# A graph network with one-hot matmuls: groups paired in TensorE's order, and 64 instead of 60 source blocks in slots

## The chip, the cores and the metric

The kernel runs on one core of a Trainium2 chip. The metric is the device time of one execution in microseconds (us). Five engines work side by side, each in its own order: TensorE (PE; its weight loads are PEld), VectorE (DVE), ScalarE (ACT), GpSimd (POOL) and SyncE (SP). SP, ACT and POOL also start DMA transfers.

## What is computed

The graph has 12500 nodes with 128 features and 200000 edges, each with 16 attributes and a type. Cut to what matters:

```
# gated layer, messages along src -> dst
msg      = x[src] @ W_msg.T + b_msg + edge_embed[type]
messages = segment_sum(msg, dst)
x        = layernorm(x + gru(messages, x))
# three layers of the second net, messages along dst -> src, plus a self loop per node
for i in 0..2:
    ee  = ea @ enc_w + enc_b
    agg = segment_sum(concat(h[dst], ee), src)      # layer 0 adds the two instead
    h   = relu(bn(agg @ w1 + b1)) @ w2 + b2         # relu between layers
out = layernorm(x + h)
```

The weights can be moved behind the sums, so each of four layers comes down to one sum of node rows over edges, `acc[target] += x[source]`, and small dense products per node. What differs between the layers is only the direction and the dense part. The graph is known only at run time, so the kernel sorts the edges on the chip first.

## The kernel before, in words

**Blocks, buckets and slots.** Nodes are in 98 blocks (NB) of 128. The edges from one source block to one target block are a bucket, some 21 edges. A bucket has SL = 32 slots. Node rows are kept as three bf16 parts side by side, 384 columns (H3). For a target block `o` the slots of its buckets are worked through in tiles of 128 slots, four buckets to a tile, and in groups of TG = 3 tiles:

- *Pick* (line 1550): four matmuls with 32 columns of weights each, one per bucket, put the source rows of the slots into PSUM: `pg`, three banks. The one-hot matrix `g` says which row a slot wants. `psg` holds two such buffers.
- *Copy* (1559, or 1556 and 1557 together): ACT, in the first layer also DVE, moves the group from PSUM to `e` in bf16. `edges` holds three such tiles.
- *Add* (1507, `scatter`): a matmul per tile with the one-hot `st` of the targets adds the slots to the 128 target rows in the bank `acc`.

The first layer (`i == 0`, the gated one) has all 98 buckets in slots: 25 tiles, 9 groups. The later layers take only the first `ic` source blocks this way, and the edges from all source blocks beyond are *fetched*: `fetch` (1484) has POOL gather `rt` tiles of 128 rows from the table in device memory with an indirect DMA each, and `scatter_rows` (1515) adds each with one matmul. The pairs (ic, rt) are in PLANS: list C, (72, 5), for layer 1; list D, (60, 7), for layers 2 and 3. `rb`, the fetched tiles in flight, is 14 minus the number of the table's resident tiles (`xf`).

**What doesn't fit.** A bucket with more than 32 edges, or a target block with more than `rt * 128` edges from beyond, has some left over. Up to 8 of the former go to the end of the last fetched tile (`held`). The rest are written to a list (C or D), and before the layer `spill` (called at 1605, body in `added`, 596 to 665) adds the list's edges in groups of 128: a hardware loop over a count read at run time, in which a position is loaded, then a place, a key and two rows are gathered, then the sum is scattered back. List A holds the overfull buckets of the first layer.

The lists are written by `Listed`. `mark` (937) counts and writes the first two rounds of list A. `rest` (1049) is a hardware loop with `count["A"][0]` turns, and each turn does one `round` (eight columns of list A) and one `more` (eight columns of list C and eight of list D). The count is the largest need of any one block, in eights:

```
V.tensor_add(self.two[:NB, q + 1:q + 2], left[:NB, 0:1], left[:NB, 1:2])   # what block and plan leave over
V.tensor_tensor(c[:, 0:1], c[:, 0:1], most, op=OP.max)                      # most = max over blocks + 7
V.tensor_single_scalar(c[:, 0:1], c[:, 0:1], 3, op=OP.logical_shift_right)  # in eights
```

`write` (1042) issues eight indirect DMAs for each eight columns. Inside the loop all three writes of a turn use the same pair of tiles `rowi` and `val`, so DVE may fill them again only once the eight DMAs have landed. All engines meet at the entry of such a loop and at the end of each turn.

**Attributes.** `attributes` gathers the 16 attributes of each edge, by the block of its `src`, 17 indirect DMAs a block (736), into one of four buffers `eat`, and `add_up` splits them in bf16 parts (753 to 757), builds a one-hot (758), and adds them up on PE (764). It is a generator, moved on by the sorting at first and then by the layers 0 and 1 at fixed places (`pace`).

**Dense part.** After the last add of a block, `finish` adds `acc` to `s` with three DVE operations (1527 to 1529; a fourth, 1531, in layer 0), and after every second block puts a generator `gru` or `gin` on the list `work`. `tick` moves it on by one stage per group: transposes of `s` (1369, 1372 or 1415), then matmuls with the weights (1385 to 1387, or 1424 and 1425), then those of 1435.

**Order.** The setup up to the lists has DVE's, ACT's and PE's orders by hand in most parts. In the layers each engine's order is chosen by the compiler's scheduler from its own estimates of time; POOL's and SP's always are. In the program text a group is picked, and then the group before it is added.

Of the kernel before, what the change touches and what calls it, by code (L numbers as in the profile page):

```python
# [8 lines left out]
F32 = mybir.dt.float32  # L9
BF16 = mybir.dt.bfloat16  # L10
# [3 lines left out]
OP = mybir.AluOpType  # L14
# [3 lines left out]
E = 200000  # L18
H = 128
# [4 lines left out]
P = 128  # L24
NB = -(-N // P)
NPAD = NB * P
H3 = 3 * H
# [21 lines left out]


IC = 72
CELL = 7
PLANS = (Plan("C", IC, 5, False, CELL + IC // 4), Plan("D", 60, CELL, True, 0))
RT = sum(p.rt for p in PLANS)
TW = CELL + IC // 4 + PLANS[0].rt
OV = 8
REF = 1 << 19

# [21 lines left out]
LW = 175  # L80
GL = 8
GE = 2
assert EP * EC == E and all(p.ic % (4 * TG) == 0 for p in PLANS)
assert LCAP >= E and (LCAP + 8 * P) // P % LW == 0
assert LR * RW >= E + NB * NQ * (RW - 1) and LR % 2 == 0

# [2 lines left out]
def gnn_kernel(ctx: ExitStack, tc: tile.TileContext, x, xT, src, dst, ea, et, w_msg, w_ihT, w_hhT, b_msg,  # L89
# [23 lines left out]
    def ctile(shape, name, dtype=F32):  # L113
        return const.tile(shape, dtype, name=name)
# [10 lines left out]
    before = ctile([P, P], "before")  # L125
    V.tensor_scalar(before, diff, 0.0, None, op0=OP.is_gt)
    after = ctile([P, P], "after")
    V.tensor_scalar(after, diff, 0.0, None, op0=OP.is_lt)
    ident = diff
    V.tensor_scalar(ident, diff, 0.0, None, op0=OP.is_equal)  # L130
    identb = ctile([P, P], "identb", BF16)
# [253 lines left out]
    pre = ExitStack()  # L385
    pst = pre.enter_context(tc.tile_pool(name="pst", bufs=2, space=PSUM))
    pss = pre.enter_context(tc.tile_pool(name="pss", bufs=2, space=PSUM))
    kp = pre.enter_context(tc.tile_pool(name="keysA", bufs=1, side="right"))
# [78 lines left out]
    nidentb = ctile([P, P], "nidentb", BF16)  # L467
    V.tensor_scalar(nidentb, ident, -1.0, None, op0=OP.mult)


# [274 lines left out]
    def add_up(b, at):  # L745
        own = owp.tile([P, EA], F32, name="own")
        nc.sync.dma_start(own, ovfe[b * P:(b + 1) * P, :])
        oh = eop.tile([P, P, WC], BF16, name="eoh")
        a3 = attr3[b % 2]
        for f0 in range(0, P, P // 2):  # L750

            if f0 == 0:
                A.copy(a3[:, :, 1:EA], at)
                V.tensor_sub(at, at, a3[:, :, 1:EA])
            else:
                A.copy(a3[:, :, EA:EA + DE], at)
# [12 lines left out]
        V.tensor_add(own[:, 1:], own[:, 1:], ps[:, EA + DE:EW])  # L769
        yield  # L770
        own6 = owp.tile([P, 6, EA], BF16, name="own6")
        pieces6(own6, own, lambda a, b: own6[:, a:b, :], lambda t, n: t[:, None, :].to_broadcast([P, n, EA]))
        pt = psa.tile([P, 1024], BF16, name="acc") if early else psd.tile([P, 1024], BF16, name="d")
# [444 lines left out]
    hs.close()  # L1218
    kb.close()

    eap = ctx.enter_context(tc.tile_pool(name="attrs", bufs=4))
    owp = ctx.enter_context(tc.tile_pool(name="own", bufs=2))
    eop = ctx.enter_context(tc.tile_pool(name="attr1h", bufs=1))
    attr3 = [eop.tile([P, WN, EW], BF16, name=f"attr3{i}") for i in range(2)]
# [78 lines left out]
    ep = ctx.enter_context(tc.tile_pool(name="edges", bufs=3))  # L1303
# [55 lines left out]
    def gru(i, b0, s):  # L1359
# [4 lines left out]
        if c1 < 2 * P:  # L1364
            V.memset(xt, 0.0)
        nc.sync.dma_start(xt[:, :c1], xT[:, b0 * P:b0 * P + c1])
        pt = psd.tile([P, 512], F32, name="d")
        for k in range(2):
            T.transpose(pt[:, k * P:(k + 1) * P], s[:, k, 0:H], ident)
            c6 = dq.tile([P, 6, NTX], BF16, name="c6")  # L1370
            pieces6(c6, s[:, k, H:], lambda a, b: c6[:, a:b, :], lambda t, n: t[:, None, :].to_broadcast([P, n, NTX]))
            T.transpose(pt[:6 * NTX, 256:384].bitcast(BF16)[:, k * P:(k + 1) * P],
                        c6.rearrange("p a b -> p (a b)"), identb)
        sT = dq.tile([P, 2 * P], F32, name="sT")
        V.tensor_copy(sT, pt[:, :256])
        cT = dq.tile([6 * NTX, 2 * P], BF16, name="cT")
# [71 lines left out]
                yield from layernorm(y, *whole, True)  # L1448


    def layer(i, pace):

        cells_only = i == 0
        p = None if cells_only else PLANS[i > 1]
# [45 lines left out]
        last = None  # L1500
        sums = {}

        def scatter(o, st, e, k):
            for j in range(min(TG, tiles - TG * k)):
                t = TG * k + j
                m = P if t < NTL - 1 else P // 2
                T.matmul(sums[o][:, :wid], st[:m, :, cell + t], e[:m, j, :wid], start=(t == 0),  # L1507
                         stop=(t == tiles - 1), skip_group_check=True)

        def scatter_rows(o, st, j0, j1):  # L1510
            if j0 >= rt:
                return
            j1 = min(j1, rt)
            for j in range(j0, j1):
                T.matmul(sums[o][:, :H3], st[:, :, row + j], fetched[o][:, j, :], start=False, stop=False,  # L1515
                         skip_group_check=True)
            if j1 == rt:
                del fetched[o]

        def finish(o):  # L1520
            nonlocal s
# [10 lines left out]
            if o % 2:  # L1532
                work.append((gru if cells_only else gin)(i, o - 1, s))

        for o in range(NB):
            g, st = ready.pop(0)
            pieces = one_hots(o + 1) if o + 1 < NB else iter(())
# [4 lines left out]
            for k in range(groups):  # L1542
# [17 lines left out]
                if cells_only:  # L1560
                    t = TG * k
                    V.tensor_tensor(e[:m, :n, H3:], iota[:m, None, :NTX].to_broadcast([m, n, NTX]),
                                    typecol[:m, o, t:t + n, None].to_broadcast([m, n, NTX]), op=OP.is_equal)
                if k == 0:
                    if last:
                        if not cells_only:
                            scatter_rows(o - 1, last[1], 2 * groups - 4, rt)
                        scatter(*last)
                        finish(o - 1)
                else:  # L1570
                    if k == 1:
                        sums[o] = psa.tile([P, 512], F32, name="acc")
                    scatter(*last)
                    if not cells_only and k > 1:
                        scatter_rows(o, st, 2 * k - 4, 2 * k - 2)
                if k == 0 and not cells_only:
                    fetch(o + rb - 1)
                last = (o, st, e, k)
                tick()
                next(pieces, None)  # L1580
                if cells_only:
                    if k in (2, 6):
                        next(chunk, None)
                    if o >= 8 and k == 4:
                        next(row_slots, None)
                if pace(o, k):
                    next(attr, None)
            for _ in pieces:
                pass
        if not cells_only:  # L1590
            scatter_rows(NB - 1, last[1], 2 * groups - 4, rt)
        scatter(*last)
        finish(NB - 1)
        while work:
            tick()
        for _ in row_slots or ():
# [2 lines left out]
    for i in range(4):  # L1599
        if i:  # L1600
            X = xtiles(-(-PLANS[i > 1].ic // XC))
            for k in range(len(X)):
                (nc.sync if k % 2 else nc.scalar).dma_start(
                    X[k], tables[i][k * XC * P:(k + 1) * XC * P, :].rearrange("(b p) f -> p b f", p=P))
        for _ in spill(i):
            pass
        layer(i, (lambda o, k: k in (1, 5) or k == 3 and o % 5, lambda o, k: k == 3)[i] if i < 2
              else lambda o, k: False)
        if i == 1:
            for _ in attr:  # L1610
                pass
# [38 lines left out]
```

## Time and profile before

Three runs: median 5781.7 us, 5779.15 to 5783.01. The profiled execution took 5775.4 us, its span 5773.6 us.

| | us |
|---|---|
| sort and lists, up to the first `finish` | 1318.5 |
| layer 0, first to last `finish` | 1487.8 (98 blocks, 15.34 each) |
| layer 1 | 1068.2 (11.01 each) |
| layer 2 | 897.7 (9.25 each) |
| layer 3 | 882.3 (9.10 each) |

The stretches run from the first to the last start of line 1529 in each layer, as the timeline has them; the 30 to 41 us between two layers are in none of the rows. Over the span PE is busy 80%, DVE 61%, ACT 59% and POOL 67%. A row of the timeline gives its start in us, its length in us, engine, line, operation, tiles, count, and in brackets the idle time before it with what ended it.

### The profile page before, as it was taken

The page shows a single profiled execution, that of the slowest core. Times are in us where ns is not written, and L with a number is a line of the kernel's source. Part 1 is how long each engine was busy: PE and PEld are TensorE (multiplying, and loading weights), DVE is VectorE, ACT ScalarE, POOL GpSimd, SP SyncE. Part 2 cuts the span into 40 slices and gives each one's busy share as a digit, 9 for nine tenths or more (in the row PEclk, how much of TensorE's full clock was granted, in tenths as well). Part 3 has the DMA queues.
Part 4 walks back from the last instruction along what each step waited for, and adds up shares of the span by engine and source line. Part 5 has one row for each costly group of instructions (what it writes and reads, how often), then busy time and mean ns, then how long its engine had stood idle before and what let it go on. Part 6 is the DMA issues. An engine that isn't in the chain of part 4 may idle for free. (4 is left out here: it accounts for less than half of the span.)

```text
span 5773.6 us, 117175 instructions
## 1 busy us (share of the span) xinstructions
PE 4590.5 (80%) x45358; PEld 2754.9 (48%) x45358; DVE 3500.1 (61%) x9502; ACT 3396.2 (59%) x4901; POOL 3855.7 (67%) x3716
## 2 busy tenths in 40 slices
PE   3874252118999999999799989988999997999998
PEld 3774122104444444444355555554555554555555
DVE  9987679837887777777444444443444443444444
ACT  7772131106666666666566666665666665666665
POOL 1001878866676767766677777775777776777776
PEclk9755555559999999999899999999999998999999
DMA  5101130012333333323444444445555555555554
GB/s 65 38 1 33 47 90 7 7 35 74 102 89 86 89 89 101 89 85 89 144 128 125 134 121 129 127 115 166 157 160 158 159 155 167 156 156 156 156 157 131
DMA packets 539973, 616.43 MB, mean 107 GB/s; under 512 B 130184, under 2 KB 458028, under 8 KB 538760
## 3 DMA queue, kind: packets, MB, share of 16 engines
q1 hardware_dynamic: 327302, 373.36, 20.1%
q0 software_dynamic: 148192, 202.82, 14.3%
q10 hardware_dynamic: 63914, 32.71, 2.7%
q8 instruction: 355, 5.82, 0.4%
q14 instruction: 210, 1.72, 0.1%
HBM read 519.72 MB, written 88.82 MB: 105 GB/s over the span
## 5 line engine op out<-in xcount | busy, mean ns | idle before, releaser
L1559 ACT CAST e<-g 128x1152 bf16<-128x1152 f32 (+1 forms) x2058 | 2216.2, 1091 | 907.7 <-PE g L1550 766.3
L1484 POOL DMA_INDIRECT x<-table,rowcol x1862 | 1861.2, 1000 | 641.4 <-issue 600.5
L736 POOL DMA_INDIRECT eat<-in_ea,eidcol x1666 | 1794.8, 1077 | 640.0 <-issue 495.0
L1550 PE MATMUL g<-x,g 128*32 128x384 bf16 x28420 | 1688.1, 333 | 93.6 <-DVE e L1557 54.2
L1507 PE MATMUL acc<-e,s 128*128 128x384 bf16 (+2 forms) x7154 | 1646.8, 344 | 116.9 <-ACT e L1556 51.6
L1507 PEld LDWEIGHTS <-s 128*128 128x128 bf16 (+1 forms) x7154 | 939.2, 153 | 745.4 <-issue 470.4
L1550 PEld LDWEIGHTS <-g 128*32 128x32 bf16 x28420 | 613.0, 96 | 911.6 <-issue 711.1
L1474 DVE TENSOR_TENSOR s<-iotas,outcol 128x704 bf16<-128x704 bf16 (+2 forms) x1568 | 838.7, 544 | 0.3 <-PE acc L1507 0.3
L1471 DVE TENSOR_SCALAR g<-inr,pidx 128x1920 bf16<-128x1920 bf16 (+2 forms) x392 | 329.9, 842 | 793.9 <-PE g L1550 685.7
L1515 PE MATMUL acc<-x,s 128*128 128x384 bf16 x1862 | 512.4, 335 | 155.5 <-DMA x<-table,rowcol 153.9
L1556 ACT CAST e<-g 128x768 bf16<-128x768 f32 x392 | 317.2, 809 | 192.9 <-PE g L1550 126.6
L567 PE MATMUL acc<-ot,oa 125*98 125x101 bf16 x1600 | 295.7, 358 | 126.8 <-ACT ot L548 95.6
L1527 DVE TENSOR_TENSOR s<-s,acc 128x128 f32<-128x128 f32 x392 | 112.5, 287 | 408.5 <-PE acc L1507 402.7
L1515 PEld LDWEIGHTS <-s 128*128 128x128 bf16 x1862 | 271.8, 146 | 176.1 <-issue 147.5
L567 PEld LDWEIGHTS <-oa 125*98 125x98 bf16 x1600 | 292.1, 277 | 129.6 <-issue 87.5
L548 ACT ACTIVATE ot<-dbb,bias 125x160 bf16<-125x160 bf16 (+2 forms) x1078 | 332.4, 406 | 16.4 <-PE acc L567 8.2
L800 POOL IOTA num<- 98x2176 uint16 x1 | 1.9, 1947 | 462.4 <-DMA sortedB<-keyB 462.4
L1427 ACT ACTIVATE gates<-d,shift,scale 128x256 f32<-128x256 f32 x294 | 150.1, 561 | 245.7 <-PE d L1425 245.7
L1557 DVE CAST e<-g 128x384 bf16<-128x384 f32 x392 | 216.6, 553 | 75.2 <-ACT e L1556 70.8
L1440 DVE TENSOR_TENSOR n<-d,b 128x256 f32<-128x256 f32 x98 | 41.6, 424 | 279.7 <-PE d L1435 278.6
L764 PEld LDWEIGHTS <-eoh 128*128 128x128 bf16 x1666 | 116.8, 163 | 197.3 <-DVE eoh L758 172.2
L316 DVE TENSOR_TENSOR keyA<-keyA 128x1024 f32<-128x1024 f32 (+1 forms) x178 | 190.9, 1072 | 15.4 <-ACT keyA L332 12.8
(423 smaller groups left out, 4761.8 us busy)
## 6 DMA issues: line engine op xcount, KB each, us to landing
inr<-inrow SPq DMA_DIRECT2D x196, 480.0 KB
inr<-inrow SPq DMA_DIRECT2D x98, 784.0 KB
inr<-inrow SPq DMA_DIRECT2D x98, 576.0 KB
x<-table,rowcol POOLq DMA_INDIRECT x1862
table<-x SPq DMA_DIRECT2D x147, 192.0 KB
eat<-in_ea,eidcol POOLq DMA_INDIRECT x1666
s<-ovf SPq DMA_DIRECT2D x147, 128.0 KB
ovf<-n SPq DMA_DIRECT2D x98, 128.0 KB
```

What stands on the lines that cost most here:

```text
L548: A.activation(self.ot[j % 2][:, b, :ENDS[j] - c0], dbb[:, c0:ENDS[j]], AF.Sign, bias=self.bias[:, b:b + 1], scale=-1.0)
L567: T.matmul(cps[:NB, :NB + NQ - 1], self.oa[c // HC][:, :, c % HC], self.ot[j % 2][:, :, c - (ENDS[j - 1] if j else 0)], start=(c == 0), st ...
L736: G.indirect_dma_start(out=at[:, t, :], out_offset=None, in_=ea, in_offset=bass.IndirectOffsetOnAxis(ap=eidcol[:, b, t:t + 1], axis=0))
L1471: V.tensor_scalar(g[:, :nb * SL], inr[:, :nb * SL], pidx, None, op0=OP.is_equal)
L1474: V.tensor_tensor(st[:, f0:f0 + P // 4, :], iotas[:, f0:f0 + P // 4, :tw], outcol[a][:, o, None, c0:c0 + tw].to_broadcast([P, P // 4, tw]) ...
L1484: G.indirect_dma_start(out=t[:, j, :], out_offset=None, in_=tables[i], in_offset=bass.IndirectOffsetOnAxis(ap=rowcol[:, o, p.kept + j:p.ke ...
L1507: T.matmul(sums[o][:, :wid], st[:m, :, cell + t], e[:m, j, :wid], start=(t == 0), stop=(t == tiles - 1), skip_group_check=True)
L1515: T.matmul(sums[o][:, :H3], st[:, :, row + j], fetched[o][:, j, :], start=False, stop=False, skip_group_check=True)
L1550: T.matmul(pg[c * SL:(c + 1) * SL, j, :H3], g[:, b * SL:(b + 1) * SL], piece(X, b), start=True, stop=True)
L1556: A.copy(e[:, :2, :H3], pg[:, :2, :H3])
L1557: V.tensor_copy(e[:, 2, :H3], pg[:, 2, :H3])
L1559: A.copy(e[:m, :n, :H3], pg[:m, :n, :H3])
```

## The change

- `ic` and `rt` of list D become 64 and 6 (CELL, the most fetched tiles, 6 instead of 7): 16 slot tiles in six groups, the last with one tile, and six fetched tiles per block in layers 2 and 3. `rb` there falls from 5 to 4.
- In all four layers PE's order is the program's (`manual_schedule` for PE), and the program picks two groups, then adds the two groups picked before; `tick` and the attributes' steps are called behind each of these adds. The generators' stages have their DVE part moved ahead of a `yield` (`pieces6` in `gru` and `add_up`). `edges` has four tiles, in a pool of its own per layer.
- `attrs` has five buffers instead of four; two constants move to a pool that is freed earlier.

```
-CELL = 7
-PLANS = (Plan("C", IC, 5, False, CELL + IC // 4), Plan("D", 60, CELL, True, 0))
+CELL = 6
+PLANS = (Plan("C", IC, 5, False, CELL + IC // 4), Plan("D", 64, CELL, True, 0))
...
-    eap = ctx.enter_context(tc.tile_pool(name="attrs", bufs=4))
+    eap = ctx.enter_context(tc.tile_pool(name="attrs", bufs=5))
...
+        c6 = dq.tile([P, 2, 6, NTX], BF16, name="c6")
+        for k in range(2):
+            pieces6(c6[:, k], s[:, k, H:], ...)
+        yield
         pt = psd.tile([P, 512], F32, name="d")
...
-        def scatter(o, st, e, k):
+        def scatter_rows(o, st, j0, j1):
+            for j in range(j0, min(j1, rt)):
+                T.matmul(sums[o][:, :H3], st[:, :, row + j], fetched[o][:, j, :], start=False, stop=False,
+                         skip_group_check=True)
+
+        def add_group(o, st, e, k):
+            if k == 0:
+                sums[o] = psa.tile([P, 512], F32, name="acc")
+            if k == groups - 1:
+                scatter_rows(o, st, 2 * k - 2, rt)
             for j in range(min(TG, tiles - TG * k)):
...
+            if 0 < k < groups - 1:
+                scatter_rows(o, st, 2 * k - 2, 2 * k)
+            if k == groups - 1:
+                fetched.pop(o, None)
+                finish(o)
...
-                if k == 0:
-                    if last:
...
-                        scatter(*last)
-                        finish(o - 1)
-                else:
...
-                    scatter(*last)
...
+                picked.append((o, st, e, k))
+                if k % 2 or k == groups - 1:
+                    for ks in range(k - k % 2, k + 1):
+                        if adding:
+                            add_group(*adding.pop(0))
+                        if ks == k:
+                            while adding:
+                                add_group(*adding.pop(0))
+                        tick()
+                        next(pieces, None)
...
+                        if pace(o, ks):
+                            next(attr, None)
+                    if k < 2:
+                        fetch(o + rb - 1)
+                    adding, picked = picked, []
...
-        layer(i, (lambda o, k: k in (1, 5) or k == 3 and o % 5, lambda o, k: k == 3)[i] if i < 2
-              else lambda o, k: False)
+        with tc.tile_pool(name="edges", bufs=4) as ep, tc.manual_schedule(engines={EN.PE}):
+            layer(i, (lambda o, k: k in (1, 5) or k == 3 and o % 5, lambda o, k: k == 3)[i] if i < 2
+                  else lambda o, k: False, ep)
```

More of the change, by code (lines that the diff above doesn't have):

```diff
@@ L51 @@
 IC = 72
[L52 to L53 removed]
+CELL = 6
+PLANS = (Plan("C", IC, 5, False, CELL + IC // 4), Plan("D", 64, CELL, True, 0))
 RT = sum(p.rt for p in PLANS)
 TW = CELL + IC // 4 + PLANS[0].rt
+TW += TW % 2
 OV = 8
@@ L82 @@
 GE = 2
-assert EP * EC == E and all(p.ic % (4 * TG) == 0 for p in PLANS)
+assert EP * EC == E and all(p.ic % 4 == 0 for p in PLANS)
 assert LCAP >= E and (LCAP + 8 * P) // P % LW == 0
@@ L124, in gnn_kernel @@
     G.iota(diff, pattern=[[1, P]], base=0, channel_multiplier=-1, allow_small_or_imprecise_dtypes=True)
-    before = ctile([P, P], "before")
-    V.tensor_scalar(before, diff, 0.0, None, op0=OP.is_gt)
     after = ctile([P, P], "after")
     V.tensor_scalar(after, diff, 0.0, None, op0=OP.is_lt)
+    kept = ExitStack()
+    kp = kept.enter_context(tc.tile_pool(name="keysA", bufs=1, side="right"))
+    before = kp.tile([P, P], F32, name="before")
+    V.tensor_scalar(before, diff, 0.0, None, op0=OP.is_gt)
     ident = diff
@@ L383, in gnn_kernel @@
     V.tensor_scalar(sel, iota[:NB, :4 * NTL].rearrange("p (t r) -> p r t", r=4), pidx[:NB], None, op0=OP.is_equal)
-    pre = ExitStack()
+    pre = kept
     pst = pre.enter_context(tc.tile_pool(name="pst", bufs=2, space=PSUM))
     pss = pre.enter_context(tc.tile_pool(name="pss", bufs=2, space=PSUM))
-    kp = pre.enter_context(tc.tile_pool(name="keysA", bufs=1, side="right"))
     total = kp.tile([NB, 1 + NQ], F32, name="total")
@@ L465, in key_a @@
         V.tensor_scalar(sgn, sgn, -2.0, 1.0, op0=OP.mult, op1=OP.add)
-    nidentb = ctile([P, P], "nidentb", BF16)
+    nidentb = kp.tile([P, P], BF16, name="nidentb")
     V.tensor_scalar(nidentb, ident, -1.0, None, op0=OP.mult)
@@ L769, in add_up @@
         V.tensor_add(own[:, 1:], own[:, 1:], ps[:, EA + DE:EW])
-        yield
+        if early:
+            yield
         own6 = owp.tile([P, 6, EA], BF16, name="own6")
         pieces6(own6, own, lambda a, b: own6[:, a:b, :], lambda t, n: t[:, None, :].to_broadcast([P, n, EA]))
+        if not early:
+            yield
         pt = psa.tile([P, 1024], BF16, name="acc") if early else psd.tile([P, 1024], BF16, name="d")
@@ L1302, in gnn_kernel @@
     ohp = ctx.enter_context(tc.tile_pool(name="onehot", bufs=2))
-    ep = ctx.enter_context(tc.tile_pool(name="edges", bufs=3))
     dp = ctx.enter_context(tc.tile_pool(name="dense", bufs=2))
@@ L1366, in gru @@
         nc.sync.dma_start(xt[:, :c1], xT[:, b0 * P:b0 * P + c1])
+        c6 = dq.tile([P, 2, 6, NTX], BF16, name="c6")
+        for k in range(2):
+            pieces6(c6[:, k], s[:, k, H:], lambda a, b: c6[:, k, a:b, :],
+                    lambda t, n: t[:, None, :].to_broadcast([P, n, NTX]))
+        yield
         pt = psd.tile([P, 512], F32, name="d")
@@ L1369, in gru @@
             T.transpose(pt[:, k * P:(k + 1) * P], s[:, k, 0:H], ident)
-            c6 = dq.tile([P, 6, NTX], BF16, name="c6")
-            pieces6(c6, s[:, k, H:], lambda a, b: c6[:, a:b, :], lambda t, n: t[:, None, :].to_broadcast([P, n, NTX]))
             T.transpose(pt[:6 * NTX, 256:384].bitcast(BF16)[:, k * P:(k + 1) * P],
-                        c6.rearrange("p a b -> p (a b)"), identb)
+                        c6[:, k].rearrange("p a b -> p (a b)"), identb)
         sT = dq.tile([P, 2 * P], F32, name="sT")
@@ L1448, in gin, with layer @@
                 yield from layernorm(y, *whole, True)
-    def layer(i, pace):
+    def layer(i, pace, ep):
         cells_only = i == 0
@@ L1508, in scatter @@
                          stop=(t == tiles - 1), skip_group_check=True)
[L1510 to L1518, printed above, removed]
+            if 0 < k < groups - 1:
[3 more added lines that the diff above has]
+                finish(o)
         def finish(o):
@@ L1533, in finish @@
                 work.append((gru if cells_only else gin)(i, o - 1, s))
+        picked, adding = [], []
         for o in range(NB):
@@ L1563, in layer @@
                                     typecol[:m, o, t:t + n, None].to_broadcast([m, n, NTX]), op=OP.is_equal)
-                if k == 0:
-                    if last:
-                        if not cells_only:
-                            scatter_rows(o - 1, last[1], 2 * groups - 4, rt)
-                        scatter(*last)
-                        finish(o - 1)
-                else:
-                    if k == 1:
-                        sums[o] = psa.tile([P, 512], F32, name="acc")
-                    scatter(*last)
[L1574 to L1587, printed above, removed]
+                picked.append((o, st, e, k))
[8 more added lines that the diff above has]
+                        next(pieces, None)
+                        if cells_only:
+                            if ks in (2, 6):
+                                next(chunk, None)
+                            if o >= 8 and ks == 4:
+                                next(row_slots, None)
+                        if pace(o, ks):
[3 more added lines that the diff above has]
+                    adding, picked = picked, []
             for _ in pieces:
                 pass
[L1590 to L1593, printed above, removed]
+        while adding:
+            add_group(*adding.pop(0))
         while work:
```

## The prediction

> **What bounds the kernel now.** I first cut the span by layers and asked for each engine's busy time there (layer 0, 1, 2, 3; PE, PEld, DVE, ACT, POOL, then PE's clock, DMA share, GB/s), then for POOL's and PE's waits in layers 2 and 3.
>
> ```profile
> 1320.00:2800.00 1480.00, 1371.33 (x14277) 690.42 (x14276) 1124.72 (x4295) 971.84 (x1432) 1033.84 (x994) 0.99 0.32 92
> 2850.00:3870.00 1020.00, 938.63 (x10036) 554.86 (x10032) 465.67 (x1214) 703.61 (x812) 781.92 (x782) 0.97 0.43 127
> 3960.00:4820.00 860.00, 787.58 (x8435) 487.80 (x8428) 382.70 (x986) 585.26 (x657) 659.76 (x658) 1.00 0.53 158
> 4890.00:5740.00 850.00, 793.52 (x8420) 484.11 (x8417) 411.44 (x1230) 559.04 (x574) 650.39 (x656) 0.99 0.52 155
> ...
> POOL x L1484 <- issue: 406.0, 1234, 30.2
> ...
> PE acc L1515 <- DMA x<-table,rowcol: 72.6, 87, 6.2
> PE d L1415 <- DVE s L1529: 36.1, 80, 0.5
> ```
>
> POOL has 0.3 us of issue before each gather and nothing else: in layer 2 it starts one every 860/658 = 1.31 us, so seven fetched tiles take 9.15 us, and a block takes 9.25. POOL sets layers 2 and 3, and PE's 72.6 us for fetched rows are its mark. In layer 1 it is the same: 1020/782 = 1.30 us a gather, without a gap, and 5 fetched tiles plus some 3.4 attribute gathers a block give 11.0, the block's time. In layer 0 POOL's 994 gathers need 1034 + 994 x 0.3 = 1332 of 1480 us. There PE comes first: busy 93%, DVE 76%. Before layer 0 everything waits for sort and lists.
>
> For PE's order I read how groups follow each other, and what stands between a block's last add and its transposes:
>
> ```profile
> 4822.28 1.16 PE L1550 MATMUL g<-x,g 128*32 128x384 bf16 x24
> ...
> 4834.45 0.67 PE L1550 MATMUL g<-x,g 128*32 128x384 bf16 x12
> 4835.05 0.71 PE L1507 MATMUL acc<-e,s 128*128 128x384 bf16 x3
> 4835.60 0.49 PE L1515 MATMUL acc<-x,s 128*128 128x384 bf16 x2
> 4836.02 0.67 PE L1550 MATMUL g<-x,g 128*32 128x384 bf16 x12
> ...
> 4822.28 0.29 DVE L1527 TENSOR_TENSOR s<-s,acc 128x128 f32<-128x128 f32 x1 [1.64 <-PE acc L1507]
> 4823.56 0.28 DVE L1529 TENSOR_TENSOR s<-s,acc 128x128 f32<-128x128 f32 x1
> 4823.89 0.33 PE L1415 MATMUL d<-ident,s 128*128 128x128 f32 x1 [0.45 <-DVE s L1529]
> ```
>
> Twelve more picks cost 1.16 - 0.67 = 0.49 us, but a group of twelve moves the next add on by 0.60: a change from picks to adds costs 0.11. Two rows before picks take 0.42 instead of 2 x 0.163: 0.09 back. So a run of picks costs 0.20 besides its work. From the adds' end to the transposed `s` pass 1.6 us, since one-hots stand between the three sums in DVE's order; the scheduler laid 24 picks into that gap.
>
> And before layer 0, the lists:
>
> ```profile
> L1044 POOL DMA_INDIRECT listA<-val,rowi x16: 966/970/1006, 1238.3 to 1267.0; - x16
>   ACT e L1556: 43.6, 1
> ...
> 1231.87 2.28 DVE L1017 MAX8 m<-same 128x8 f32<-128x2048 f32 x1
> 1234.33 2.27 DVE L1018 MATCH_REPLACE8 same<-m,same 128x2048 f32<-128x2048 f32 x1
> ...
> 1272.18 0.96 POOL L791 DMA_INDIRECT cells<-sortedA,start  x1 [0.30 <-issue]
> 1276.91 0.37 SPq L608 DMA_DIRECT2D pos<-listA  x1
> 1283.58 0.98 POOL L621 DMA_INDIRECT key<-sortedA,pos  x1 [0.30 <-issue]
> 1285.95 0.15 DVE L625 TENSOR_SCALAR neg<-key 128x1 int32<-128x1 int32 x1 [4.34 <-DMA key<-sortedA,pos]
> ```
>
> Line 1044 ran 16 times, the two rounds that `mark` writes. So the loop of `rest` made no turn, and nothing ran in the spill loops. A copy waits 43.6 us meanwhile: work of layer 0 does not pass these loops.
>
> **The change part by part.** *64 buckets, 6 tiles: what no longer fits.* I counted the buckets of the reference's inputs (its default seed). With (60, 7) the fullest target block has 892 edges from beyond, under 896, and nothing is left over. With (64, 6) the mean is 703, but four blocks exceed what they hold: 775, 772, 813 and 768 against 768. 61 edges are left over, 46 of them in block 71. So list D has one group of 128, and the list loop makes (46 + 7) >> 3 = 6 turns. Before: (0 + 7) >> 3 = 0.
>
> One turn, from the rows: MAX8, MATCH_REPLACE8 and the small operations to `rowi`: 5.3 us. Then eight list writes of A: seven starts 1.28 apart (0.97 + 0.30), and from the eighth's start 2.37 until another engine uses the result (1283.58 to 1285.95): 11.3. DVE fills `rowi` and `val` again, three small operations, 0.6. C the same, 11.9. D: 7 x 1.28, then to the first instruction after the meeting of all engines 4.7 (1272.18 to 1276.91): 13.7. Sum 5.3 + 11.3 + 0.6 + 11.3 + 0.6 + 13.7 = 42.8; six turns **257 us**, nothing beside it. If DVE's part hid and landings were free, 3 x 10.2 + 4.7 = 35 (212 us); if every landing took the 4.7 us, 48 (285). The Trainium skill (DMA: Bandwidth & Descriptors, "Anatomy of one DMA — SWDGE (gpsimd) path") gives an indirect DMA a fixed 2.0 us, against 2.37 here: with it 6 x 2 x 0.37 = 4 us less. I take the row.
>
> The spill group in each of layers 2 and 3 is a chain: position, place, key, the two rows (2.37 each, the second row 1.28 later), small DVE and PE work 5, scatter and meeting 4.7: 4 x 2.37 + 1.28 + 5 + 4.7 = 20.5. It stands where all engines wait for POOL's first gather, whose rows need that same meeting; two layers **+41** (30 to 55).
>
> *Layers 2 and 3.* POOL: six gathers, 7.85 us a block, no longer the bound. PE per block, starts from the timeline: 16 tiles of picks x 0.154, 22 adds and rows x 0.163, three runs of picks x 0.20 (four before), dense part 1.3: 2.46 + 3.59 + 0.6 + 1.3 = 7.95. But PE's order is now fixed: after every second block the two transposes stand directly behind the last add and wait the 1.6 us shown above, with all picks behind them, and so ACT's next copy. In the other blocks only four adds (0.65 us) stand between two pairs of picks, while two copies take 2 x 1.12: the fourth group's picks wait some 0.7 for its buffer, the adds after them 0.3 more for `acc`. Stepping through two blocks (b: 1.03 picks, to the transposes 2.46, 0.2, picks 1.03, adds 1.31, line 1424's stage 1.18, picks 0.72, adds 1.69, line 1435's stage 0.98 = 10.6; a: 1.03, copy-bound to 3.5, 1.4, 0.72, 1.78 = 7.4) gives 18.0 per two, with PE's slow windows (clock 0.99) 9.1 per block instead of 9.25 and 9.10: **-15** for 196 blocks. From both sides: the bare 7.95 would be -235; 0.5 us more per block of waiting +100.
>
> *Edits at nothing.* `rb` 4 instead of 5: tiles are asked for three blocks, some 27 us, ahead of use, and POOL needs 7.85 for them; with POOL still the bound it would cost PE's 73 us again. One more resident tile (672 KB) to load per layer lies beside the spill chain. The fourth `e` tile, `c6` for two blocks, `pieces6` ahead of a `yield` add no work; DVE is idle 24% in layer 0 and over half of the time later. SP's and POOL's orders stay the scheduler's; `fetch` comes a pair of groups later in the text, 3 us of 27.
>
> *Layer 1.* Stays with POOL. The fifth buffer lets POOL's order hold 17 attribute gathers before the `cells` gathers instead of in the layers: 17 x 1.30 = **-22** here, and before layer 0, where DVE waits 38 us for those `cells` and POOL has no gap since the sort, 17 x 1.25 = **+21**. A queue shift, no gain.
>
> *Layer 0.* Runs of picks fall from 9.5 to 5 per block (read off both kernels' orders): 4.5 x 0.20 = 0.9 us a block, -88. Against that, the transposes stand behind the four sums and the eight DVE operations of `pieces6`, at 0.2 each and with one-hots between: 2 to 3.4 us per two blocks, 1.35 a block, of which before cost 0.3: +1.0. And PE's present waits for copies (DVE `e` L1557 above all, some 80 us) partly fall into that stall. I take **-60**; POOL's 1332 us is the floor (-155), +60 the other end.
>
> A rule that speaks against the fixed order: the Trainium skill (TensorE: Matmul & The Clock Gate, "Part 1: The HAM clock gate") lets PE's clock fall to half after an idle window of 3.4 us. The row has 0.97 to 1.00 in the layers, and the stalls counted are 1.6 to 3.4 us. By the row they cost what they last; by the rule, if layer 0's stall reached the window, each would slow the next 3.4 us: 49 x 1.7 = +83. I follow the row and keep that for the upper end.
>
> Sum: 257 + 41 - 15 - 22 + 21 - 60 = **+222**. The profiled execution took 5775.4 (span 5773.6): 5997. The runs' median is 6 us above it: 6003, given as **6005 us**.
>
> **The rivals.** *The lists stay empty* (0.05): other inputs, all blocks within 768. Then no turn and no group: 5782 - 76 = 5706. This is the other side, and it decides early: a single turn and its spill groups cost 43 + 41 and use up the 76. For it: the profile shows no counts. Against: the counts of the default inputs, which agree with zero turns before. *PE follows its bare work* (0.15): ticks hide the transposes, layer 0 reaches POOL's floor and layers 2 and 3 come halfway to 7.95: 257 + 41 - 1 - 155 - 115 = +27, 5809; halfway to that, 5905. For it: POOL was the bound in three layers. Against: nothing stands between add and transposes. *The fixed order costs more* (0.12): layer 0 +60, layers 2 and 3 +100: 257 + 41 - 1 + 160 = +457, 6238; halfway 6120. For it: DVE is 76% busy in layer 0, and what it delays now holds up all of PE. Main course: 0.68.
>
> **The numbers.** Main course alone 5930 to 6080: turns 35 to 48 us (-45, +28), spills (-11, +14), layers +-60. The range takes in half of the second and third rival: 5885 to 6120. 0.2% (12 us) is what a measurement of this kernel tells from none. Faster: the first rival and a few in a hundred of the second, 0.08; same 0.02; slower 0.90.
>
> **What would show it.** Line 1044's successor: 16 + 6 x 24 = 160 instructions; layer 0's first copy held 280 to 330 us instead of 44; one scatter to `ovf` at the start of each of layers 2 and 3; POOL in layers 2 and 3 with gaps beyond 0.3; PE waiting for DVE's last sum 1.4 us or more before transposes. Wrong if the list rows stay at 16, or if blocks in layers 2 and 3 come under 8.7 or layer 0 under 13.9.

## The result and the profile after

The changed kernel takes **6468.0 us** (median of four runs, 6466.19 to 6470.56) against 5781.3 us of the kernel before: ratio 1.1188, 95% interval 1.1169 to 1.1208. It is slower, as forecast, but by 687 us where 223 were forecast, and the range of 5885 to 6120 does not hold it.

The spans differ by 694 us (6467.9 and 5773.6). By stages, each from the first to the last `finish` of a layer:

| us | before | after | difference | forecast |
|---|---|---|---|---|
| up to the first `finish` | 1318.5 | 1687.6 | +369 | +278 |
| layer 0 | 1487.8 (15.34 a block) | 1690.3 (17.43) | +202 | -60 |
| layer 1 | 1068.2 (11.01) | 1109.7 (11.44) | +41 | -22 |
| gap ahead of layer 2, of layer 3 | 35.2, 30.0 | 61.0, 53.6 | +26, +24 | +20.5 each |
| layer 2 | 897.7 (9.25) | 915.6 (9.44) | +18 | -15 for both |
| layer 3 | 882.3 (9.10) | 897.5 (9.25) | +15 | |

The same stretches as before, layer 0 to 3 (busy us of PE, PEld, DVE, ACT and POOL, each with its number of instructions, then PE's granted clock, DMA share, GB/s):

```profile
1690.00:3370.00 1680.00, 1351.13 (x14290) 745.39 (x14291) 1148.89 (x4306) 960.00 (x1432) 1023.36 (x997) 0.91 0.29 81
3420.00:4500.00 1080.00, 887.13 (x10145) 582.37 (x10142) 480.84 (x1231) 701.01 (x821) 821.55 (x786) 0.97 0.41 122
4600.00:5500.00 900.00, 794.41 (x8943) 522.38 (x8945) 401.24 (x999) 617.37 (x763) 543.46 (x570) 1.00 0.49 147
5560.00:6450.00 890.00, 798.20 (x9009) 525.88 (x9008) 424.18 (x1253) 593.71 (x682) 562.78 (x576) 1.00 0.48 144
```

In layer 0 no engine is a bound any more: PE falls from 93% busy to 80%, DVE from 76% to 68%, and PE's clock from 0.99 to 0.91. What PE waits for there, and then in layer 2 what PE and POOL wait for (who waited, for whom, us in total, how often, the longest):

```profile
PE d L1378 <- DVE s L1541: 103.2, 48, 4.4
PE d L1379 <- DVE c L728: 68.6, 49, 2.1
PE g L1563 <- DVE e L1570: 43.0, 49, 3.2
...
PE d L779 <- DVE n L1397: 20.4, 18, 1.4
PE d L766 <- DVE n L1397: 20.1, 18, 1.1
...
PE d L1422 <- DVE s L1541: 73.9, 47, 1.6
...
POOL x L1492 <- PE acc L1513: 178.7, 82, 2.9
```

1378, 1379 and 1422 are the transposes; each pair of blocks now waits there for DVE. 779 and 766 are the attributes' transpose and sums. POOL's 178.7 us are the gaps that were to show that it is no longer the bound of layer 2.

The list writes (line 1049, before 1044), with the shortest, median and longest in ns and the first and last start, who waited for them (us, times), and the wait of layer 0's first copy:

```profile
L1049 POOL DMA_INDIRECT listA<-val,rowi x64: 963/970/1014, 1262.3 to 1629.0; - x64
L1049 POOL DMA_INDIRECT listC<-val,rowi x48: 964/969/973, 1291.2 to 1593.8; - x48
L1049 POOL DMA_INDIRECT listD<-val,rowi x48: 964/970/972, 1308.6 to 1611.1; - x48
...
  DVE rowi L1038: 187.5, 12
...
  DMA ovf<-cur,to: 416.0, 1
```

64 + 48 + 48 = 160 writes: the six turns are there. But the copy is held 416 us, not 280 to 330.

On two chips the kernel before itself took 8333 and 8564 us. `apart` and `buf5` ran only there; of them only ratios to it, and what their traces show ahead of layer 0, are used. Six more kernels ran both there and elsewhere. Their results below are from elsewhere; the ratios on the two chips were 1.0316 (`later`), 1.0311 (`by_hand`), 1.0385 (`warm`), 0.9616 (`free60`), 0.9777 (`best`) and 0.9809 (`best_4`). The same code begins layer 0 there 6 to 55 us later.

### The profile page after: what moved, and what is told of

Same layout as the page of the kernel before. It is cut to its first block, busy times and chain, and to the rows that moved or that the text cites. A ratio compares the mean times of both kernels' runs of the same rounds, so it can differ in the third digit from the quotient of the medians.

```text
span 6467.9 us, 119697 instructions
## 1 busy us (share of the span) xinstructions
PE 4476.1 (69%) x46148; PEld 2892.5 (45%) x46148; DVE 3610.0 (56%) x9728; ACT 3418.8 (53%) x5095; POOL 3789.2 (59%) x3673
## 5 line engine op out<-in xcount | busy, mean ns | idle before, releaser
L1572 ACT CAST e<-g 128x1152 bf16<-128x1152 f32 (+1 forms) x2254 | 2254.0, 1041 | 879.9 <-PE g L1563 803.9
L1492 POOL DMA_INDIRECT x<-table,rowcol x1666 | 1647.6, 989 | 808.6 <-issue 447.6
L1563 PE MATMUL g<-x,g 128*32 128x384 bf16 x29204 | 1539.5, 339 | 512.2 <-DVE g L1479 383.4
L1524 PE MATMUL acc<-e,s 128*128 128x384 bf16 (+1 forms) x7350 | 1624.5, 348 | 88.8 <-DVE s L1541 61.0
L1524 PEld LDWEIGHTS <-s 128*128 128x128 bf16 x7350 | 964.5, 150 | 661.7 <-issue 406.9
L1563 PEld LDWEIGHTS <-g 128*32 128x32 bf16 x29204 | 700.5, 98 | 1184.3 <-issue 522.2
L1482 DVE TENSOR_TENSOR s<-iotas,outcol 128x832 bf16<-128x832 bf16 (+1 forms) x1568 | 861.2, 552 | 0.0
L1479 DVE TENSOR_SCALAR g<-inr,pidx 128x2048 bf16<-128x2048 bf16 (+2 forms) x392 | 336.7, 859 | 738.5 <-PE g L1563 723.7
L1513 PE MATMUL acc<-x,s 128*128 128x384 bf16 x1666 | 420.6, 327 | 37.8 <-DMA x<-table,rowcol 37.5
L1513 PEld LDWEIGHTS <-s 128*128 128x128 bf16 x1666 | 240.3, 144 | 62.4 <-issue 29.7
L1422 PE MATMUL d<-ident,s 128*128 128x128 f32 x294 | 88.6, 304 | 227.9 <-DVE s L1541 226.5
```

The lines of the kernel that those rows point to most:

```text
L1479: V.tensor_scalar(g[:, :nb * SL], inr[:, :nb * SL], pidx, None, op0=OP.is_equal)
L1482: V.tensor_tensor(st[:, f0:f0 + P // 4, :], iotas[:, f0:f0 + P // 4, :tw], outcol[a][:, o, None, c0:c0 + tw].to_broadcast([P, P // 4, tw]) ...
L1492: G.indirect_dma_start(out=t[:, j, :], out_offset=None, in_=tables[i], in_offset=bass.IndirectOffsetOnAxis(ap=rowcol[:, o, p.kept + j:p.ke ...
L1563: T.matmul(pg[c * SL:(c + 1) * SL, j, :H3], g[:, b * SL:(b + 1) * SL], piece(X, b), start=True, stop=True)
L1572: A.copy(e[:m, :n, :H3], pg[:m, :n, :H3])
```

## The experiments

Two theories. The first: the left-over edges cost some 400 us (list loop and spills), and PE's fixed order costs the rest, because PE now stands still where DVE is late. The rival: the pairs, the sizes or the fifth buffer cost the layers' time, and the order by hand is harmless.

### The sizes, undone and alone

`after_60x7` is the changed kernel, `before_64x6` the kernel before, each with the other's sizes (the latter with the assert and `TW` as in the change):

```
# after_60x7
-CELL = 6
-... Plan("D", 64, CELL, True, 0))
+CELL = 7
+... Plan("D", 60, CELL, True, 0))
# before_64x6: the same lines the other way round
```

> The changed kernel with the sizes of the last two layers as before: 60 buckets, 7 fetched tiles, so nothing is left over. Theory 1 (the left-over edges cost the list loop and two spill groups, the rest is PE's fixed order): the stretch before layer 0 loses some 350 us, the two gaps ahead of layers 2 and 3 some 50; layers 2 and 3 have POOL as the bound again, 9.3 to 9.5 us a block, no change or +30. In all 6050 to 6110 us, still 270 to 330 above the kernel before. Rival (the left-over costs only what was forecast, 298, and layer 0 suffers from something else that the sizes bring): 6170 or more.

> The kernel before with only the sizes of the last two layers changed to 64 buckets and 6 fetched tiles; pairs, order by hand and the fifth attribute buffer are not there. Theory 1: list loop +350, spill groups +50; layers 2 and 3, where POOL needs only 7.85 us a block now, gain 0.3 to 0.6 us a block (-60 to -120); layers 0 and 1 as before. In all 6060 to 6120 us. Rival (the list loop is dear only because the changed kernel's order around it is): under 6000.

`after_60x7` took 6044.4 us (1.0453 of before, 1.0435 to 1.0470): layer 0 starts at 1350.2, the gaps are 37.2 and 28.7, layer 0 stays at 17.39 us a block. So the left-over costs 337 us ahead of layer 0 and some 49 in the gaps, and has nothing to do with layer 0.

`before_64x6` took 6223.4 us (1.0760, 1.0742 to 1.0778), more than expected: list loop +345 (1663.7), gaps +22 and +21.5, as expected; but layers 2 and 3 did not gain 60 to 120 us, they lost 36 (9.48 and 9.24 us a block). Its layer 2:

```profile
4350.00:5260.00 910.00, 867.34 (x9008) 505.39 (x9001) 383.88 (x1007) 640.92 (x767) 584.56 (x573) 1.00 0.51 148
```

PE is busy 95% of it at a granted clock of 1.00. Sixteen tiles are six groups instead of five, and picked and added group by group PE has no room for the sixth. With 64 buckets and no pairs PE takes POOL's place as the bound.

### The order by hand, taken away

```
# after_free
-        with tc.tile_pool(name="edges", bufs=4) as ep, tc.manual_schedule(engines={EN.PE}):
+        with tc.tile_pool(name="edges", bufs=4) as ep:
# after_free0: without it for i == 0 only
```

> The changed kernel with the order by hand of TensorE taken away in all four layers: pairs, sizes and fifth buffer stay, and the scheduler lays TensorE's instructions. Theory 1 (it is the fixed order that makes TensorE wait for VectorE's sums and pieces): layer 0 comes back to 15.0 to 15.5 us a block, layers 1 to 3 to 11.0, 9.0, 8.9 or better: 6190 to 6230 us. Rival (the pairs themselves, or the fifth buffer, cost the time): layer 0 stays above 17 us a block, 6400 or more.

> The changed kernel with the order by hand taken away in layer 0 alone. Theory 1: layer 0 gives back its 200 us (15.0 to 15.5 us a block, granted clock 0.98 or more), layers 1 to 3 stay: 6250 to 6290 us. Rival (layer 0 is slow through the fifth buffer or the pairs): 6440 or more.

`after_free` 6059.9 us (1.0479, 1.0461 to 1.0496), `after_free0` 6206.3 (1.0732, 1.0714 to 1.0750). Layers 0, 2 and 3 of `after_free`:

```profile
1700.00:3100.00 1400.00, 1280.07 (x14254) 728.27 (x14254) 1116.69 (x4280) 947.64 (x1426) 1056.65 (x986) 0.99 0.35 96
...
4310.00:5150.00 840.00, 793.94 (x8922) 520.89 (x8920) 404.79 (x997) 611.22 (x760) 545.13 (x569) 1.00 0.53 157
5220.00:6040.00 820.00, 789.28 (x8898) 519.49 (x8900) 422.68 (x1237) 580.96 (x673) 555.10 (x569) 1.00 0.53 155
```

The fixed order costs 408 us of the 687: by layers 275.6, 17.2, 59.4 and 59.9. Without it layer 0 needs 14.58 us a block, less than before the change (15.34), and layers 2 and 3 8.83 and 8.64. In layers 0, 2 and 3 the pairs, with these sizes, are a gain (in layer 0 the buffers have no part in it: `best_4` below has 14.61 with four); the order by hand gives it back and more. I had expected less of it (6190 to 6230). Where the scheduler orders PE, the transposes' waits in layer 0 shrink from 172 us to 31; the longer of the two rows in `after_free0`:

```profile
PE d L1378 <- DVE s L1541: 28.0, 47, 1.4
```

### Is it the fixed order, or where the transposes stand in it?

`by_hand` is the kernel before with PE's order by hand in the text's order and nothing else. `later` is the changed kernel with two more `yield`s ahead of the transposes in `gru` and in `gin`, so that a pair of picks stands between.

```
# by_hand
+        with tc.manual_schedule(engines={EN.PE}):
             layer(i, (lambda o, k: ...
# later, in gru and in gin
+        yield
+        yield
         pt = psd.tile([P, 512], F32, name="d")
```

> The kernel before with TensorE's order by hand in the four layers, in the order of its text; no pairs, no other size, four attribute buffers. Run again for the same reason. Theory 1 (a fixed order costs by itself, mostly in layer 0): layer 0 at 17 to 19 us a block instead of 15.3, in all 6050 to 6250 us. Rival (the order by hand hurts only together with the pairs): under 5850.

> The changed kernel with the transposes of each pair of blocks laid two steps later in TensorE's fixed order (two more yields ahead of them in the dense parts of all layers). Run again, since the chip of the first run had the kernel before itself at 8333 us. Theory 1 (the fixed order costs because the transposes stand where VectorE's sums and pieces are not ready): most of the 408 us that the scheduler's order gives comes back, layer 0 at 15.0 to 15.6 us a block with a clock of 0.97 or more, layers 2 and 3 at 8.8 and 8.6: 6100 to 6160 us. Rival (a fixed order makes TensorE wait for whatever is late next, as the copies or the attribute steps): 6300 or more, with the wait in another row.

`by_hand` took 6316.4 us (1.0932, 1.0914 to 1.0950), more than expected: 18.51, 11.95, 9.95 and 9.78 us a block. Its waits in layer 0 are those of the changed kernel:

```profile
PE d L1369 <- DVE s L1529: 89.9, 48, 2.6
PE d L1372 <- DVE c L726: 66.0, 48, 2.2
```

So the fixed order costs without pairs too. `later` took 6074.5 us (1.0510, 1.0492 to 1.0527), 394 less than the changed kernel, and as fast as the scheduler's order to 15 us. Layers 2 and 3 fell to 8.40 and 8.42, below what the scheduler reached. This is the only wait of PE left in its layer 2:

```profile
PE g L1567 <- ACT e L1576: 16.8, 48, 0.4
```

A fixed order is not bad in itself: it lacks distance behind DVE's sums. Layer 0 came back to 15.49, not to 14.58; there PE waits 77 us for the copies' DVE half and 70 at the attributes' steps, the rows that the rival named, and 35 at adds for the last sum. So two steps are not enough in all places of layer 0, and a part of the rival holds there.

### The clock

`warm` puts twelve matmuls of no use ahead of the transposes of `gru`; they are written over.

```
         pt = psd.tile([P, 512], F32, name="d")
+        for _ in range(12):
+            T.matmul(pt[:, :H3], identb, piece(X, 0), start=True, stop=True)
```

> The changed kernel with twelve matmuls of no use (identity by a piece of X, some 2 us by the rows) ahead of the transposes of each pair in layer 0; they fill most of the 2.1 us for which TensorE waits there and are written over. Run again for the same reason. Theory 1 with the clock (it falls in the stall, 0.91 over layer 0, and the work behind it runs slower): clock in layer 0 at 0.96 or more, layer 0 faster by 30 to 80 us although work was added: 6390 to 6440 us. Rival (the clock in the record follows the idle time and costs nothing by itself): no gain, 6470 to 6530.

6413.1 us (1.1096, 1.1078 to 1.1115), 55 less than the changed kernel; layer 0 alone 1624.5, that is 66 less, with 49 x 12 matmuls more. Its layer 0, and its waits at the two kinds of transposes there:

```profile
1700.00:3320.00 1620.00, 1375.78 (x14908) 785.08 (x14907) 1146.05 (x4311) 955.36 (x1435) 1034.34 (x997) 0.97 0.31 84
...
PE d L1381 <- DVE c L728: 69.1, 48, 2.3
...
PE d L1380 <- DVE s L1543: 11.3, 9, 2.5
```

The wait for `s` went from 103.2 to 11.3 us because work fills it, and the clock from 0.91 to 0.97. The other waits stay (69.1 us for `c`, 68.6 without the matmuls), so the only thing this gives to the work behind is speed. How one such stall looks in the changed kernel:

```profile
1839.51 0.15 DVE L1543 TENSOR_TENSOR s<-s,acc 128x10 f32<-128x10 f32 x1
...
1839.64 0.48 PE L1378 MATMUL d<-ident,s 128*128 128x128 f32 x1 [3.17 <-DVE s L1541]
...
1841.86 0.15 DVE L728 TENSOR_TENSOR c<-s,c 128x10 bf16<-128x10 f32 x1
...
1842.07 0.31 PE L1379 MATMUL d<-identb,c 128*60 128x128 bf16 x1 [1.95 <-DVE c L728]
...
1843.49 2.11 PE L1563 MATMUL g<-x,g 128*32 128x384 bf16 x24
...
1849.90 1.16 PE L1563 MATMUL g<-x,g 128*32 128x384 bf16 x24
```

PE stands 3.17 us, then 1.95, and the next 24 picks take 2.11 us instead of 1.16; 6 us later they are fast again. The 10 us from 1840 have a granted clock of 0.57:

```profile
1840.00:1850.00 10.00, 7.14 (x42) 3.01 (x45) 5.54 (x21) 4.27 (x6) 5.01 (x6) 0.57 0.22 52
```

This is the rule that the prediction weighed and set aside: the Trainium skill (TensorE: Matmul & The Clock Gate, "Part 1: The HAM clock gate") has a slow default state that about 3.4 us of activity releases, and an idle window of that length brings back. Here idle stretches of 3.17 and 1.95 us with one transpose between were enough. By the row of before the clock was to cost nothing, by the rule up to 83 us (the prediction's estimate from that page); `warm` got back 66.

### The list loop

`apart` gives each list its own `rowi` and `val` tiles, so that DVE fills C's rows while A's writes are still on their way.

```
-            self.written = [(t(f"rowi{n}", 8, I32), t(f"val{n}", 8, I32)) for n in range(3)]
+            self.written = [(t(f"rowi{n}", 8, I32), t(f"val{n}", 8, I32)) for n in range(5)]
...
             for q, p in enumerate(PLANS):
+                self.rowi, self.val = self.written[3 + q]
```

> The changed kernel with index and value tiles of their own for each of the three lists, so that within a turn VectorE fills the next list's rows while the writes of the one before are still landing. Theory 1 (two waits of 7.5 us a turn for landed writes): a turn falls from 58 to 60 us to 43 to 46, and POOL issues its 24 writes without a gap; 6 turns give back 75 to 95 us: 6375 to 6395 us. Rival (the queue works the writes off that slowly, and the meeting at the turn's end waits for what is left): less than 40 us, 6430 or more.

A turn of the changed kernel, at its writes' ends: the last write to A and DVE's next `rowi`, the last write to D and the next turn:

```profile
1282.80 0.97 POOL L1049 DMA_INDIRECT listA<-val,rowi  x1 [0.31 <-issue]
1290.26 0.17 DVE L1038 TENSOR_TENSOR rowi<-row,spare 128x8 int32<-128x8 f32 x1 [16.23 <-DMA listA<-val,rowi]
...
1317.51 0.97 POOL L1049 DMA_INDIRECT listD<-val,rowi  x1 [0.30 <-issue]
1328.46 2.30 DVE L1022 MAX8 m<-same 128x8 f32<-128x2048 f32 x1 [20.06 <-PEq L1057]
```

1290.26 - 1282.80 = 7.46 us until the eight writes have landed, and 10.95 from the last write to D to the next turn (9.06 in a later one). The meeting of all engines stands there, at a turn's end, and where the loop is left. At its entry the trace shows none: DVE starts the first turn at 1267.79, while POOL still issues the writes before it.

What the DMA engines do in these 7.46 us:

```profile
1282.80:1284.60 1.80, 0.00 (x0) 0.00 (x0) 0.00 (x0) 0.00 (x0) 0.97 (x1) 0.50 0.03 1
1284.60:1290.20 5.60, 0.00 (x0) 0.00 (x0) 0.00 (x0) 0.00 (x0) 0.00 (x0) 0.50 0.00 0
```

After 1.8 us no packet is on them any more, and DVE waits 5.6 us longer for word that the write is done. Not every indirect write to device memory is so late: behind the spill group's scatter of 128 rows of 512 bytes the next instruction starts 3.06 us after it (4326.80 to 4329.86 in `before_64x6`). Why single words take longer stays open.

In `apart`, POOL issues its 24 writes without a gap:

```profile
1345.95 0.97 POOL L1050 DMA_INDIRECT listC<-val,rowi  x1 [0.30 <-issue]
...
1365.04 0.96 POOL L1050 DMA_INDIRECT listD<-val,rowi  x1 [0.30 <-issue]
1374.19 2.29 DVE L1022 MAX8 m<-same 128x8 f32<-128x2048 f32 x1 [36.13 <-PEq L1058]
```

A turn takes 43.9 to 44.2 us after the first. The changed kernel has 58.2 to 58.5, and `later`'s code, with the list loop unchanged, has 59.9 to 60.9 on the other of the two chips told of above. So the two waits a turn for landed writes cost 14 to 17 us, in six turns some 85 to 100. (Layer 0 starts at 1618.1 here and at 1704.1 there, 86 us apart, but between chips that start differs by up to 55 us for the same code.) And the end of a turn comes 9.1 to 11.0 us after the last of 24 writes in a row, no later than after the last of eight: it is the delay of a write, not a queue that fills up. In all `apart` took 8750.2 us (1.0207 of the kernel before on that chip, 1.0172 to 1.0242); the changed kernel has no run on that chip, so what the whole gains is not measured.

### What is left, and the kernel that beats both

`free60` is `after_60x7` with the scheduler's order: of the change, pairs and the fifth buffer remain. `buf5` is the kernel before with the fifth buffer alone.

```
# free60
-CELL = 6
-... Plan("D", 64, CELL, True, 0))
+CELL = 7
+... Plan("D", 60, CELL, True, 0))
-        with tc.tile_pool(name="edges", bufs=4) as ep, tc.manual_schedule(engines={EN.PE}):
+        with tc.tile_pool(name="edges", bufs=4) as ep:
# buf5
-    eap = ctx.enter_context(tc.tile_pool(name="attrs", bufs=4))
+    eap = ctx.enter_context(tc.tile_pool(name="attrs", bufs=5))
```

> The changed kernel with 60 buckets and 7 fetched tiles, and with the scheduler's order on TensorE: pairs and the fifth buffer are what is left of the change. Run again for the same reason; there it took 0.962 of the kernel before. Sum of the stages measured so far: before layer 0 as with the old sizes (1350), layer 0 14.6 us a block, layer 1 11.1, layers 2 and 3 between 8.7 (TensorE) and 9.15 (seven gathers of POOL): 5640 to 5720 us, faster than both kernels. Rival (POOL's seven gathers hold layers 2 and 3 above 9.2): 5730 or more.

> The kernel before with the fifth attribute buffer alone (and the two constants moved that make room for it). Theory 1 (a shift in POOL's queue, no gain): layer 0 starts 21 to 32 us later, layer 1 takes 0 to 22 us less, layers 0, 2 and 3 as before: 5780 to 5815 us. Rival (the buffer lets layers 0 and 1 run freer by more than it costs ahead of them): 5770 or less.

`free60` took 5743.5 us (0.9941, 0.9925 to 0.9958): 0.6% faster than before, but by less than I expected (5640 to 5720); the rival had the size. Layers 2 and 3 stay at 9.24 and 9.09 us a block, and POOL's waits in layer 2 say why:

```profile
POOL x L1492 <- issue: 180.9, 594, 0.3
POOL x L1492 <- PE g L1563: 11.6, 38, 0.3
```

0.3 us before each gather and next to nothing else: with seven gathers POOL is the bound, pairs or not, as read before the change. Six gathers alone make PE the bound (`before_64x6`), pairs alone leave POOL; together they pay.

`buf5` gave 0.9984 (0.9969 to 0.9998), next to nothing, and only on a chip where the layers take more than half as long again, so it decides little; `best` against `best_4` below does.

`best` has 68 buckets and 6 tiles (by a count of the inputs' edges the fullest block then fits, so nothing is left over), pairs, PE's order by the scheduler in layer 0 and by hand in the others, with `later`'s two steps in `gin`. `best_4` is the same with four attribute buffers.

```
-PLANS = (..., Plan("D", 64, CELL, True, 0))
+PLANS = (..., Plan("D", 68, CELL, True, 0))
...
-        with tc.tile_pool(name="edges", bufs=4) as ep, tc.manual_schedule(engines={EN.PE}):
+        with tc.tile_pool(name="edges", bufs=4) as ep, (tc.manual_schedule(engines={EN.PE}) if i else ExitStack()):
```

> Put together from the findings: 68 buckets and 6 fetched tiles in the last two layers (all blocks fit, nothing left over), pairs, TensorE's order by the scheduler in layer 0, by hand in layers 1 to 3 with the transposes two steps later, five attribute buffers. Sum of the stages: 1350 ahead of layer 0, layer 0 1415, gaps 41, 37, 29, layer 1 1073 to 1080, layers 2 and 3 at 8.4 plus one tile of picks and one of adds (0.32) = 8.7 us a block, 845 each, end 12: 5640 to 5660 us. Rival (17 tiles bring back a bound in layers 2 and 3): above 5720.

> The same with four attribute buffers. If the fifth only shifts POOL's queue: layer 0 starts 30 us earlier (1319), layer 1 gives back part of it: 5620 to 5650 us. If the pairs need the fifth buffer in layers 0 and 1: layer 0 above 14.9 us a block and 5670 or more.

`best` 5665.1 us (0.9810, 0.9794 to 0.9827), `best_4` **5649.5 us** (0.9779, 0.9763 to 0.9795 of the kernel before). The stages of `best` were to sum to 5640 to 5660: layer 0 14.59 us a block, layer 1 11.06, layers 2 and 3 8.75 each, where 8.7 was expected. Its layers 2 and 3:

```profile
3930.00:4780.00 850.00, 823.82 (x9496) 562.37 (x9496) 416.50 (x1013) 652.71 (x769) 553.77 (x571) 1.00 0.54 165
4810.00:5640.00 830.00, 808.03 (x9363) 550.86 (x9355) 435.38 (x1242) 617.45 (x674) 566.68 (x572) 1.00 0.51 157
```

PE is busy 97% at a granted clock of 1.00, so this is PE's work. The fifth buffer starts layer 0 24 us later (1350.1 against 1325.9) and gives 4 us back in layer 1.

## Why the prediction was off, by its steps

The forecast of +222 fell 472 us short of the +694 between the spans: 91 ahead of layer 0, 262 in layer 0, 63 in layer 1, 9 in the gaps and 48 in layers 2 and 3.

*The count of the left-over, and that nothing hides it: right.* Six turns, 160 writes, one group in each of layers 2 and 3, zero before.

*The price of a turn, 42.8 us: too low.* It measured 58.2 to 58.5 after the first turn's 60.7. The sum had 2.37 us for each of two landings, from the row of a gather, and 4.7 for the meeting, from a gather followed by one; the writes take 7.46 and 9.1 to 11. That is 2 x 5.1 + 5 = 15 us a turn, the whole difference. The two-sided bound failed for the same reason: its upper end took 4.7 us, a delay behind a gather, as the most a landing could cost.

The rows of before held the right price. Its list loop made no turn, but the engines met where it is passed:

```profile
1247.26 0.97 POOL L1044 DMA_INDIRECT listA<-val,rowi  x1 [0.30 <-issue]
...
1257.32 0.29 DVE L1104 SCALAR_TENSOR_TENSOR sm<-valid,sl 98x128 bf16<-98x128 bf16 x1 [13.93 <-ACTq L669]
```

This meeting came 10.1 us after the last list write and 8.8 after the one gather behind it. The second, which the prediction read, came 9.9 us after the last list write (1267.0 to 1276.91, both in its rows) and 4.7 after the last gather. Timed from the gathers the two disagree; timed from the writes they agree, with each other and with the 9.1 to 11 of the changed kernel. The prediction timed the meeting from the gather alone. The Trainium skill (DMA: Bandwidth & Descriptors, "Anatomy of one DMA — SWDGE (gpsimd) path"), weighed for its 2.0 us, says in the same section that the completion of a DMA can be surprisingly late when it writes to device memory; the 5.6 us without a packet agree with that, and the spill's scatter (3.06 us in all) shows that it need not be so. The loop cost 345 us (`before_64x6`), not 257.

*Spill groups, 20.5 us each: right.* 22 and 21.5 in `before_64x6`, and by its steps too: from the load of the position to the layer's first gather 21.0 us (4309.84 to 4330.83), of them 4.0 for scatter and meeting.

*Cells later by 21 us: right*, 24 from `best` against `best_4`. *Layer 1, -22: wrong.* The 17 gathers did leave the layer, but the fifth buffer gives back only 4. The order by hand adds 17 (`after_free`). The sizes alone add 22 in layer 1 (`before_64x6`), though list C is as it was: there POOL's gathers take 1.02 us each instead of 1.00, some 16 us for 803 of them. Why stays open.

*Layer 0, -60: wrong in sign, +202.* The gain from longer runs was there: 88 us forecast, 73 measured (`after_free` against before; the scheduler leaves 6.7 runs of picks a block there, not 5, so not all of it need come from the runs). PE's waits for copies were to shrink as well: -88, +98 and a result of -60 leave 70 of their 80 us for that, and they only fell from 84 to 46 us. The largest row of before, 43.0 in the changed kernel:

```profile
PE g L1550 <- DVE e L1557: 53.6, 80, 1.6
```

The stall was sized at +1.0 us a block; the fixed order costs 2.84. Three things make that up (1.45, 0.7 and 0.6), as far as the waits show. The transposes' waits are 172 us against 31 with the scheduler's order (28.0 + 3.1), 1.45 a block, where 1.0 was said. The attributes' steps on PE, counted among edits that "add no work", wait too: 74 us in five rows (20.4, 20.1, 15.5, 9.1, 9.1), 0.7 a block more. And "I follow the row and keep that for the upper end" was the wrong choice on the clock. The row of 0.99 came from a kernel whose order kept PE busy (93%), and the change took just that away. In the changed kernel the picks within runs of 24, and the adds, stand further apart than their usual spacing by 37 and 35 us in sum, against 7 and 4 in `after_free0`. So the clock costs some 60 us, and `warm` got back 66.

*Layers 2 and 3, -15: wrong, +33.* The stall was sized well: 73.9 us for 47 pairs, 1.57 each where 1.6 was said. PE's bare work was not: `later`, with 17 us of waits, needs 8.40 us a block, not 7.95, and so two blocks took 18.9 and 18.5 where the steps came to 18.0. The wait for a copy's buffer was half of what was said (17.3 us in 50 times, 0.35 each, not 0.7). (The bound of -235 for the bare 7.95 would be -240 by its own numbers.) The gain was real all the same: sizes and pairs together give 86 us with the scheduler's order, and the order by hand takes 119 (59.4 + 59.9).

The rival "the fixed order costs more" had the mechanism in its one sentence, that what DVE delays now holds up all of PE, but with +60 for layer 0. The range ended at half of it, and the whole of it, 6238, would still have been 230 us short.

## What to carry to other kernels

A fixed order on an engine must leave distance where it takes another engine's result: ask for each such place how long the other engine needs with its whole queue, and lay that much work of one's own between; here two steps more gave back 394 of 408 us in all, but in layer 0 only 187 of 276. A stall is priced with what it does to TensorE's granted clock (here some 60 of 276 us), not by the clock of a kernel that has no stalls. A loop over left-overs is priced by the fullest block, not by the number of edges (61 edges cost 345 us and two spills); and a wait for a write is timed from the row of a write, here 9.9 us and not 4.7.

## What the runs showed of the hardware

- Eight indirect writes of 128 single words to device memory were landed 7.46 us after the last one's start, though no packet was on the DMA engines for the last 5.6 us. A hardware loop's next turn began 9 to 11 us after its last such write, with eight or 24 in a row. A scatter of 128 rows of 512 bytes was passed in 3.06 us.
- The granted clock fell to 0.57 over 10 us after waits of 3.17 and 1.95 us with one transpose between; filling the first with useless matmuls made layer 0 66 us faster.
- On two chips the kernel before took 8333 and 8564 us. The stretch ahead of layer 0 was nearly as on the others (1344 us in `buf5`), a copy lasted the same (mean 1091 ns in `buf5` and in before), but the mean granted clock was 0.785 instead of 0.894, and ACT stood idle before its copies 2824 us instead of 908, 1385 us of it for a releaser that the profile could not name. The cause stays open.
